# A seven-product cross-attention kernel: other signs in the sums, the softmax sum folded from T3, product 6 of y in blocks, and an earlier place for GpSimd's sums

## The chip, the cores and the metric

The kernel runs on one core of a Trainium2 chip. The metric is the device time of one execution in microseconds (us). The core's engines work side by side, each through its own list of instructions: TensorE (PE in the profile, with its weight loads as PEld) does matrix products into PSUM, VectorE (DVE) works on pairs of tensors, ScalarE (ACT) copies, scales and takes exponentials, GpSimd (POOL) reduces over partitions and issues DMAs that can add to their target, and SyncE (SP) issues plain DMAs. GpSimd's DMAs are the queue q0 of the profile and SyncE's are q1.

## The reference

There are eight batches. For each of them, in fp32:

```python
q = einsum('bcn,dc->bnd', x1, Wq) + bq                 # x1: 512 x 1024, q: 1024 x 64
k = einsum('bcn,dc->bdn', x2, Wk) + bk[:, None]        # x2 = ctx: 512 x 1024, k: 64 x 1024
v = einsum('bcn,dc->bdn', x2, Wv) + bv[:, None]        # v: 512 x 1024
attn = softmax(einsum('bnd,bdm->bnm', q, k), axis=2)   # 1024 x 1024
out = einsum('bcm,bnm->bcn', v, attn) + x1
```

## The kernel before

**What is computed.** The value projection comes after the attention: with e the exponentials of the scores less their maximum, laid out as m x n, the kernel computes y = x2 · e (512 x 1024 x 1024), divides y by the sums of e over m, and then forms out = Wv · y + bv + x1 (512 x 512 x 1024). In these words "context" is x2, its transposed blocks are the tiles `a`, and the weights are `w`.

**The seven-product form.** Both large products, "y" (context times e) and "o" (Wv times y), are cut into 2 x 2 blocks and done with seven block products in place of eight, in Winograd's form. The left factors are 11, 12, 22 and the sums S1 to S4, the right ones 11, 21, 22 and the sums T1 to T4. A table gives for each product its factors, its PSUM banks and whether it opens them; products that do not open a bank add to what stands there:

```python
MULT = {1: ("11", "11", "a", True), 2: ("12", "21", "c", True), 6: ("S2", "T2", "a", False),
        7: ("S3", "T3", "c", True), 5: ("S1", "T1", "a", False), 3: ("S4", "22", "a", False),
        4: ("22", "T4", "c", False)}
```

Blocks of e carry half 0 or 1 of the n columns as their second index, and half 0 or 1 of the m rows as their first: 11 and 21 belong to half 0, 12 and 22 to half 1. Before the change S1 = 21 + 22, S2 = 11 - S1, S3 = 11 - 21, S4 = 12 + S2 on the left (`left_sums`, lines 101 to 111), and T1 = 12 - 11, T2 = T1 - 22, T3 = 22 - 12, T4 = 21 + T2 on the right (`right_sums`, line 317). For y the left sums are those of the context, new in every batch: S1 is loaded (line 155) and added to by a DMA (159), S3 and S2 are negated on ACT (167) and added to by a DMA (171), and S4 is a DVE sum (108). T3 is made in place, on ACT and by a DMA (341, 342), T4 by copies on ACT and a DMA (330, 336).

**Two ways of doing one product.** `multiply` (line 420, matmuls at 437) is the plain one: per 128 rows of the result, four matmuls of 512 columns. `multiply_seeded` (lines 595 to 628) cuts the block product once more into seven, over 256 columns each, in the order 1, 7, 6, 2, 5, 4, 3 (its "steps"): steps 1, 6 and 5 chain in one PSUM tile (`ps_i...chain`), step 7 has its own (`ps_i...third`), ACT copies the chain's states into the banks (line 611) and step 7 into an SBUF tile `v`, and `complete` on DVE adds `v` to the second bank (626). Such a product needs sums of its own: four of the left factor, `left_stream` (line 485, tiles `aI`), and three passes for the right one, `right_stream` (500 over 1024 elements, 505 and 507 over 512 each; tiles `eI`). The digit in `ps_i5chain` or `eI7yT` is that of the product. Before the change all products of y are done in this way in batches 2 to 8, except product 6; batch 1 does 1, 2 and 6 plain. In the o stage product 7 is in blocks, woven with the plain 5 and 3 (`multiply_57`, lines 545 to 593); 1, 6, 2 and 4 are plain.

**One period.** `period` (line 868 on) writes the work for batch s from product 1 of its y to the last eviction of its output, with the scores and the softmax of the next batch n between, and loads for the ones after that (nn, nnn). A manual schedule holds: each engine executes its instructions strictly in the order in which they are written. The code numbers batches 0 to 7, the text 1 to 8. `five` stands for the batches in the middle: neither the first nor the last two. The order of PE in a middle period is product 1, 2, 6 of y, the scores of half 0 of batch n, products 5, 7, 3, the scores of half 1 and the keys of later batches, product 4, and then the o stage: 1, 6, 2, the woven 5, 7, 3, and 4. The periods meet at product 1.

**Softmax.** For each half h, DVE folds the maximum over four score tiles (`fold`, line 248), POOL takes it over the partitions (`highest`, 264), DVE subtracts it (`lower`, 299; tiles `e<-e,top`), ACT takes the exponential (308), and the sum of e over m comes from three fold passes on DVE or, for half 0, from DMAs that add (`add_tile`, 724), from a last fold of the two halves of the tile, and from POOL's all-reduce (`total`, 266 to 273). `invert` and `spread` (275 to 284) bring the reciprocal to all partitions, `scale_y` (648) multiplies y by it.

**Evictions.** `evict_y` (652) and `evict_t3` (638) form y's blocks from banks and the copies `u1`, `u6`, `u7`; `evict_o` (670 to 721) adds bias, copies and banks to the output tile, POOL then adds x1 by DMA (720), and SP stores it (721). Both DMAs are written right behind the eviction. `uo5` (tag `u5`) is the copy of product 5 of the o stage, into which block 22 of the output is built.

Of the kernel before, what the change touches and what calls it, by code (L numbers as in the profile page):

```python
# [15 lines left out]
def kernel(  # L16
# [84 lines left out]
    def left_sums(a, *ks):  # L101

        for k in ks:
            if k == "S3":
                nc.vector.tensor_tensor(a["21"], a["11"], a["21"], ALU.subtract)
                a["S3"] = a["21"]
            elif k == "S4":
                nc.vector.tensor_tensor(a[k], a["12"], a["S2"], ALU.add)
            else:
                x, y, op = {"S1": ("21", "22", ALU.add), "S2": ("11", "S1", ALU.subtract)}[k]  # L110
                nc.vector.tensor_tensor(a[k], a[x], a[y], op)
# [154 lines left out]
    def total(s, h):  # L266
        fold_halves(s, h, ALU.add)
        s.den[h] = sb.tile([P, H], F32, tag="den", name=f"den_{s.b}_{h}", bufs=2)
# [45 lines left out]
    def right_sums(t, k):  # L314

        x, y = {"T1": ("12", "11"), "T2": ("T1", "22"), "T3": ("22", "12"), "T4": ("21", "T2")}[k]
        nc.vector.tensor_tensor(t[k], t[x], t[y], ALU.add if k == "T4" else ALU.subtract)
# [8 lines left out]
    def copy_t4(s):  # L326

        s.t["T4"] = t4 = sb.tile([P, MH, H], F32, tag="eT4", name=f"eT4_{s.b}")
        for i in (0, 2):
            nc.scalar.copy(t4[:, i : i + 2, :], s.t["21"][:, i : i + 2, :])  # L330
# [7 lines left out]
    def sum_t3(s, i):  # L338

        t3 = s.t["T3"][:, i : i + 2, :]  # L340
        nc.scalar.mul(t3, t3, -1.0)
        nc.gpsimd.dma_start(t3, s.t["22"][:, i : i + 2, :], accum_op=ALU.add)

    def copy_u1(s, j):
        if j == 0:
            s.tmp[1] = sb.tile([P, 2, H], F32, tag="yT1", name=f"uy1_{s.b}")
        nc.scalar.copy(s.tmp[1][:, j, :], s.bank["a", j])
# [51 lines left out]

    def iter_t4(s):  # L400
        sum_y(s, "T4")
        yield
# [126 lines left out]
    def inner_parts(s, i):  # L529

        ks = ("third", "chain") if i in (2, 7) else ("chain", "third")
        of = {k: ps_s.tile([P, 2, H], F32, tag="sc", name=f"ps_i{i}{k}_{s.b}")[:, 0, left] for k in ks}
        return of["chain"], of["third"]
# [61 lines left out]
    def multiply_seeded(s, i, v_tag, hooks={}, bank=None):  # L595
# [11 lines left out]
        v = sb.tile([P, 2, H], F32, tag=v_tag, name=f"v{i}_{s.b}")[:, 0, left]  # L607
# [16 lines left out]
        def complete():  # L624
            b = b1.rearrange("p (a n) -> p a n", a=2)
            nc.vector.tensor_tensor(b, b, v.unsqueeze(1).to_broadcast([P, 2, H // 2]), ALU.add)
# [6 lines left out]
    def copy_7(s, j):  # L633
        if j == 0:
            s.tmp[7] = sb.tile([P, 2, H], F32, tag="u1", name=f"uy7_{s.b}")
        nc.scalar.copy(s.tmp[7][:, j, :], s.bank["c", j])
# [15 lines left out]
    def evict_y(s, k):  # L652

        bank, add = RESULT[k]
        if k == "22" or s.b == B - 1 and k == "21":
            bank, add = "a", 6
        s.y[k] = y = sb.tile([P, 2, H], F32, tag=f"y{k}", name=f"y{k}_{s.b}")
        for j in range(2):
            nc.vector.tensor_tensor(y[:, j, :], s.bank[bank, j], s.tmp[add][:, j, :], ALU.add)
# [10 lines left out]
    def evict_o(s, k):  # L670
# [37 lines left out]
        if add is None:  # L708
            o = sb.tile([P, 2, H], F32, tag="u1" if k == "11" else "r", name=f"r{k}_{s.b}")
            for j in range(2):  # L710
                nc.scalar.activation(o[:, j, :], s.bank[bank, j], AF.Identity, bias=bias(j))  # L711
        else:
# [6 lines left out]
        if k != "21":  # L719
            nc.gpsimd.dma_start(o, block(s, k, x1), accum_op=ALU.add)  # L720
        nc.sync.dma_start(block(s, k, out), o)
# [146 lines left out]
    def period(s, n, nn, nnn):  # L868
# [25 lines left out]
        def scores_0():  # L894
            then = scores_and(n, 0, 1 if nn else 2, "c", next_queries if nn else nothing)
            if nn is None:
                first(6, (1,))
            if s.b:
                for i in range(1, MH):
                    fold(n, 0, i, "max", ALU.max)  # L900
                highest(n, 0)
            return then
# [4 lines left out]

        def first_sum():
# [3 lines left out]
        open_t(s)  # L912
        if s.b == 0:
# [6 lines left out]
            s.a["S4"] = sb.tile([P, MH, C // 2], F32, tag="aS4", name=f"aS4_{s.b}")  # L920
            nc.scalar.copy(s.a["S4"], s.a["S2"])
            nc.gpsimd.dma_start(s.a["S4"], x2T[s.b, 0, 1], accum_op=ALU.add)
# [12 lines left out]
            for i in range(1, MH):  # L935
                fold(s, 1, i, "sum", ALU.add)
            total(s, 1)
            sum_e(s, "T3")
            weave(right_stream(s, 5, s.t["T1"], "y21", "u5"))
# [25 lines left out]
        else:  # L965
            complete_1 = multiply_seeded(s, 1, "y11")
            sum_e(s, "T1", "T2")
            complete_1()
            sums_5 = left_stream(s, 5, s.a["S1"], "i2"), right_stream(s, 5, s.t["T1"], "y21", "u1")
            if n:  # L970
                weave(folds(s, 1, "sum", ALU.add), left_stream(s, 7, s.a["S3"], "yT4"))
                total(s, 1)
                invert(s, 0)
            else:
                weave(folds(s, 1, "sum", ALU.add), left_stream(s, 7, s.a["S3"], "yT4"))
                weave(*sums_5)
            complete_2 = multiply_seeded(
                s, 2, "y22", {5: lambda: copy_u1(s, 0), 4: lambda: copy_u1(s, 1)}
            )
            sum_t3(s, 0)  # L980
            sum_t3(s, 2)
            if n is None:
                total(s, 1)
            complete_2()
            evict_y(s, "11")
            copy_t4(s)
            add_t4(s)
            first(6, (0,) if n and nn is None else range(2))
            if n:
                weave(*sums_5)  # L990
            if n:
                sum_a(s, "S4")
                evict_q = scores_0()
                spread(s, 0)
                shares(s, 1)
            if n:
                weave(right_stream(s, 7, s.t["T3"], "yT1", "yT2"), left_stream(s, 3, s.a["S4"], "aI3"))
            else:
                sum_a(s, "S4")
                weave(right_stream(s, 7, s.t["T3"], "yT1", "yT2"), left_stream(s, 3, s.a["S4"], "aI3"))  # L1000
                invert(s, 0)
                spread(s, 0)
# [4 lines left out]
            if n is None:  # L1007
                shares(s, 1)
            if n:
                weave(right_stream(s, 3, s.t["22"], "eT1"), lowers(n, 0, 0, 1))  # L1010
# [8 lines left out]
            if n:  # L1019
                lower(n, 0, 1)  # L1020
            complete_3 = multiply_seeded(s, 3, "r", hooks, "c")
# [6 lines left out]
            if n:  # L1028
                for i in range(2, MH):
                    lower(n, 0, i)  # L1030
            complete_3()
            evict_t3(s)
        if n:
            if s.b:
                load_a(n, "11")
            begin_s1(n)
# [15 lines left out]
            end_s1(n)  # L1052
            if nn:
                next_keys()
        if late and n:
            weave(left_stream(s, 4, s.a["22"], "a12"), right_stream(s, 4, s.t["T4"], "eT2"))
        if late:
            scale_y(s, "11", "T3", "22")
# [3 lines left out]
        if five:  # L1062
            weave(folds(n, 1, "max", ALU.max))
# [8 lines left out]
        if five:  # L1072
            highest(n, 1)
        complete_4()
        if late and n:
            negate(n, "S3")
# [10 lines left out]
        scale_y(s, "21")  # L1087
        if s.b == 0:
# [4 lines left out]
        if five:  # L1093
            weave(iter_t4(s), right_stream(s, "o7", s.y["T3"], "eT1"))
# [4 lines left out]
        if late and n and not five:  # L1099
            weave(folds(n, 1, "max", ALU.max), right_stream(s, "o7", s.y["T3"], "eT1"))  # L1100
# [11 lines left out]
        second(6)  # L1112
        if n:
# [8 lines left out]
        evict_o(s, "11")  # L1122
        if n:
            if not five:
                add_tile(n, 0, 3)
            if late:
                inner_left(n, 1, n.a["11"], "i2")
        if late:
            complete_7, rest = multiply_57(s)
        else:  # L1130
# [4 lines left out]
        if n:  # L1135
            for i in range(MH) if s.b else (2,):
# [5 lines left out]
        if n:  # L1142
            negate(n, "S2")
            add_11(n, "S2")
        evict_o(s, "22")
# [3 lines left out]
        if n:  # L1149
            weave(  # L1150
                right_stream(n, 1, n.e[0][:, 0], "yT1", "yT2"), left_stream(n, 2, n.a["12"], "aS4")
# [4 lines left out]
            evict_o(s, "12")  # L1156
# [46 lines left out]
```

## Time and profile before

| what | value |
|---|---|
| median of 3 runs | 677.41 us (676.89 to 677.58) |
| the profiled execution's own time | 677.15 us |
| its span in the profile | 675.4 us |
| largest groups of DVE: lowering the scores (299) | 60 instructions, 70.6 us |
| folding (248), maximum alone | 30 instructions, 36.7 us |
| exponentials on ACT (308) | 60 instructions, 61.5 us |
| POOL's all-reduces: sums (269), maxima (264) | 52.5 us and 31.0 us |
| plain y products and product 6 (437, `ps_ya<-eT,aS`) | 112 matmuls, 49.5 us |

The span goes from the first to the last instruction; the execution's own time is 1.75 us longer. An engine's "busy" time says nothing of who sets the time, since engines run side by side; that is read from what each waits for, stage by stage. In what follows, a line of a "windows" view gives for a stretch of the span its length, then each engine's busy time with the number of instructions, the clock that was granted to TensorE (1.00 is full), the mean busy share of the 16 DMA engines, and GB/s. A line of a "groups" view gives the source line, engine, operation and tile, the count, the busy time, the mean duration in ns, and the idle time ahead with what ended it. A line of a "timeline" view gives start and busy time in us, engine, line, operation, tiles, the count, and in square brackets the wait ahead of it and what ended that.

### The profile page before, as it was taken

How to read it: one execution, taken by the hardware profiler on the slowest of the kernel's cores; microseconds unless marked ns; L12 is line 12 of the kernel's file. 1: busy time of each engine (PE TensorE's matmuls, PEld its weight loads, DVE VectorE, ACT ScalarE, POOL GpSimd, SP SyncE). 2: the span in 40 equal slices, each digit the busy share in tenths (PEclk: the TensorE clock that was granted, in tenths of full speed). 3: DMA queues.
4: the chain of work that ended last, by engine and by line, in shares of the span. 5: the costliest groups of instructions: out<-in, count | busy, mean ns of one | idle time of the engine just before them, and what ended most of it. 6: DMA issues, size and time to landing. Idle time of an engine off the chain costs nothing.

```text
span 675.4 us, 7565 instructions
## 1 busy us (share of the span) xinstructions
PE 666.4 (99%) x2510; PEld 413.1 (61%) x2510; DVE 612.5 (91%) x811; ACT 358.5 (53%) x619; POOL 218.2 (32%) x188
## 2 busy tenths in 40 slices
PE   8999999999999999999999999999999999999996
PEld 5334754766556665657656486574855757566853
DVE  1999999999999889998999979999899989999984
ACT  3755456366465464654745647445565456565321
POOL 0126206260344411642134411445122460153400
PEclk9999999999999999999999999999999999999999
DMA  9678798958997959969599695996969968489412
GB/s 304 272 207 278 190 264 152 247 116 245 249 212 192 196 172 301 173 184 249 152 276 190 179 267 151 240 214 175 270 108 222 218 136 231 94 154 251 80 42 98
DMA packets 51638, 134.26 MB, mean 199 GB/s; under 512 B 5648, under 2 KB 7952, under 8 KB 51600
## 3 DMA queue, kind: packets, MB, share of 16 engines
q0 software_dynamic: 23328, 57.75, 47.9%
q1 hardware_dynamic: 27984, 75.64, 31.0%
q10 hardware_dynamic: 288, 0.39, 0.2%
q8 instruction: 20, 0.33, 0.2%
q14 instruction: 18, 0.15, 0.1%
HBM read 88.35 MB, written 16.81 MB: 156 GB/s over the span
## 4 chain that ended last, share of the span: by engine, by line
PE 87%; DVE 7%; DMA 3%; POOL 1%; issue 1%; SPq 1%; ACT 0%; DVEq 0%; POOLq 0%
PE ps_yc L518 10%; PE ps_ya L437 7%; PE ps_oa L559 6%; PE ps_ya L518 5%; PE ps_oa L437 5%; PE ps_s L228 5%; PE ps_o L437 4%; PE ps_oc L437 4%; PE ps_o L457 4%; PE ps_q L181 4%; PE ps_k L181 3%; PE ps_i4chain L518 3%; PE ps_i5chain L518 3%; PE ps_i7chain L518 3%; PE ps_i3chain L518 3%; PE ps_i1chain L518 2%
## 5 line engine op out<-in xcount | busy, mean ns | idle before, releaser
L269 POOL PARTITION_ALL_REDUCE den<-sum x16 | 52.5, 3283 | 72.7 <-DVE few L277 52.6
L724 POOL DMA_DIRECT2D sum<-e x21 | 27.9, 1328 | 145.7 <-ACT sum L729 71.6
L299 DVE TENSOR_TENSOR e<-e,top 128x1024 f32<-128x1024 f32 x60 | 70.6, 1218 | 0.4 <-POOL top L264 0.4
L308 ACT ACTIVATE e<-e 128x1024 f32<-128x1024 f32 x60 | 61.5, 1055 | 8.4 <-DVE e L299 7.8
L237 ACT COPY e<-ps_s 128x1024 f32<-128x1024 f32 x46 | 45.7, 1031 | 8.3 <-PE ps_s L228 8.3
L437 PE MATMUL ps_ya<-eT,aS 128*128 128x512 f32 x112 | 49.5, 593 | 0.0
L228 PE MATMUL ps_s<-q,k 64*128 64x512 f32 x188 | 47.5, 609 | 0.8 <-ACT q L751 0.8
L264 POOL PARTITION_ALL_REDUCE top<-max x16 | 31.0, 1940 | 52.1 <-DVE few L277 20.4
L248 DVE TENSOR_TENSOR max<-max,e 128x1024 f32<-128x1024 f32 x30 | 36.7, 1225 | 2.5
L437 PEld LDWEIGHTS ps_ya<-eT,aS 128*128 128x128 f32 x112 | 21.2, 190 | 24.1 <-issue 23.5
L284 POOL DMA_DIRECT2D den<-row x16 | 9.0, 561 | 78.0 <-DMA row<-few 75.0
L228 PEld LDWEIGHTS ps_s<-q,k 64*128 64x128 f32 x188 | 16.8, 186 | 24.8 <-issue 16.3
L720 POOL DMA_DIRECT2D r<-in_x_dram x14 | 29.3, 2090 | 2.9 <-ACT r L711 2.9
L648 DVE TENSOR_TENSOR y<-y,den 128x1024 f32<-128x1024 f32 x24 | 29.3, 1220 | 0.2
L437 PE MATMUL ps_o<-y,w 128*128 128x512 f32 x64 | 28.8, 592 | 0.0
L457 PE MATMUL ps_o<-y,w 128*128 128x512 f32 x64 | 28.8, 592 | 0.0
L437 PE MATMUL ps_oa<-yT,w_S 128*128 128x512 f32 x64 | 28.8, 592 | 0.0
L437 PE MATMUL ps_oc<-yT,w 128*128 128x512 f32 x64 | 28.8, 592 | 0.0
L611 ACT COPY ps_yc<-ps_i7chain 128x256 f32<-128x256 f32 x32 | 11.4, 357 | 30.3 <-PE ps_i7chain L518 22.3
L611 ACT COPY ps_ya<-ps_i5chain 128x256 f32<-128x256 f32 x32 | 11.4, 358 | 29.9 <-PE ps_i5chain L518 25.7
L485 DVE TENSOR_TENSOR aI<-a,aI 128x256 f32<-128x256 f32 x60 | 26.0, 433 | 1.0
L611 ACT COPY ps_ya<-ps_i1chain 128x256 f32<-128x256 f32 x28 | 10.0, 357 | 30.6 <-PE ps_i1chain L518 27.0
(257 smaller groups left out, 1734.8 us busy)
## 6 DMA issues: line engine op xcount, KB each, us to landing
x_in_x_dram<-in_x_dram SPq DMA_DIRECT2D x60, 512.0 KB, 9.3
a<-in_x2T_dram SPq DMA_DIRECT2D x32, 512.0 KB, 9.5
sum<-e POOLq DMA_DIRECT2D x21, 512.0 KB, 7.5
eT<-eT POOLq DMA_DIRECT2D x16, 512.0 KB, 10.9
aS<-in_x2T_dram POOLq DMA_DIRECT2D x15, 512.0 KB, 7.4
uo<-in_x_dram POOLq DMA_DIRECT2D x14, 512.0 KB, 9.6
r<-in_x_dram POOLq DMA_DIRECT2D x14, 512.0 KB, 11.5
out_dram<-r SPq DMA_DIRECT2D x14, 512.0 KB, 3.4
```

The source lines that it names most:

```text
L181: nc.tensor.matmul(ps[r, :], w_sb[:, c, :], s.x[:, c, ts(h, H)], start=(c == 0), stop=(c == CT - 1),)
L228: nc.tensor.matmul(ps[g], s.k[r, ts(i, P)], s.q[r, ts(h, H)], start=True, stop=True)
L237: nc.scalar.copy(e[:, :, i, :], whole)
L248: nc.vector.tensor_tensor(f, e[:, :, 0, :] if i == 1 else f, e[:, :, i, :], op)
L269: nc.gpsimd.partition_all_reduce(s.den[h], s.mx[h][:, 0, :], P, ReduceOp.add)
L299: nc.vector.tensor_tensor(e, e, top, ALU.subtract)
L308: nc.scalar.activation(e, e, AF.Exp)
L437: nc.tensor.matmul(ps[:, n], left[ka][:, k, ts(j, P)], right[kb][:, k, n], start=opens and k == 0, stop=i in (2, 3, 4) and k == n_k - 1, s ...
L457: nc.tensor.matmul(ps, w["11"][:, k, ts(j, P)], s.y["11"][:, k, :], start=k == 0, stop=False, skip_group_check=True)
L518: nc.tensor.matmul(ps, s.inner[i][ka][:, k, :], s.inner[i, "t"][kb][:, k, :], start=opens and k == 0, stop=z in (2, 3, 4) and k == n_k - 1 ...
L559: nc.tensor.matmul(ps[:, n], w[ka][:, k, ts(j, P)], s.y[kb][:, k, n], start=False, stop=i == 3 and k == 1, skip_group_check=True,)
L611: nc.scalar.copy(out, of)
```

## The change

It has four parts.

1. *Signs.* The second block column of the context and the second block row of e carry the opposite sign inside the form: S1 = 21 - 22, S2 = 11 - S1, S4 = 12 - S2; T1 = 12 - 11, T2 = T1 + 22, T3 = 22 + 12, T4 = T2 - 21. S1 is now begun by ACT's negation of 22 and not by a load. T3 needs no negation. The copies of T4 and of product 7 are negated, and the eviction of 21 subtracts.
2. *The sum of half 1.* T3 = 22 + 12 is already the sum of both row blocks of half 1; `sum_1` folds it in one DVE pass and the last fold of halves, in place of three passes over four tiles.
3. *Product 6 in blocks.* In batches 3 to 6 (`s.six`) product 6 of y goes through `multiply_seeded`. It has its own `left_stream` and `right_stream`; S4 is made by ACT's negation of S2 and a DMA that adds, ACT copies `uy6` behind the scores (`copy_u6`), a DMA adds `uy1` to it, and the closing addition works on `uy6`. `uy1` and some sums move to other tiles.
4. *Order.* In the middle batches the next batch's T1 and the DMAs for T3 are written in the output stage, ahead of the eI1 sums and of the x1 additions of blocks 22 and 12. These two additions and their stores leave `evict_o` as functions (`leave`); that of 22 is called behind T3's DMAs, that of 12 in the next period behind T2. The exponentials of half 1 are taken earlier: two during the eviction of block 11, two behind `multiply_57`. The lowering of the scores, the scaling of y and the folds change places; so do the sums for product 4 in batch 7 and the reciprocal of half 0 in batch 8.

```diff
-            nc.vector.tensor_tensor(a[k], a["12"], a["S2"], ALU.add)
+            nc.vector.tensor_tensor(a[k], a["12"], a["S2"], ALU.subtract)
...
+            self.six = 2 <= b < B - 2
...
+    def copied_s4(s):
+        s.a["S4"] = sb.tile([P, MH, C // 2], F32, tag="aS4", name=f"aS4_{s.b}")
+        nc.scalar.mul(s.a["S4"], s.a["S2"], -1.0)
+    def add_s4(s):
+        nc.gpsimd.dma_start(s.a["S4"], x2T[s.b, 0, 1], accum_op=ALU.add)
     def begin_s1(s):
-        nc.sync.dma_start(s.a["S1"], x2T[s.b, 1, 0])
+        nc.scalar.mul(s.a["S1"], s.a["22"], -1.0)
     def end_s1(s):
-        nc.gpsimd.dma_start(s.a["S1"], x2T[s.b, 1, 1], accum_op=ALU.add)
+        nc.gpsimd.dma_start(s.a["S1"], x2T[s.b, 1, 0], accum_op=ALU.add)
...
+    def sum_1(s):
+        t = s.t["T3"]
+        s.mx[1] = sb.tile([P, 2, H], F32, tag="fold", name=f"sum_{s.b}_1", bufs=2)
+        nc.vector.tensor_tensor(s.mx[1], t[:, 0:2, :], t[:, 2:4, :], ALU.add)
+        fold_halves(s, 1, ALU.add)
+    def total_1(s):
+        sum_1(s)
+        reduce_total(s, 1)
...
     def sum_t3(s, i):
         t3 = s.t["T3"][:, i : i + 2, :]
-        nc.scalar.mul(t3, t3, -1.0)
         nc.gpsimd.dma_start(t3, s.t["22"][:, i : i + 2, :], accum_op=ALU.add)
+    def copy_u6(s, j):
+        if j == 0:
+            s.tmp[6] = sb.tile([P, 2, H], F32, tag="u6", name=f"uy6_{s.b}")
+        nc.scalar.copy(s.tmp[6][:, j, :], s.bank["a", j])
...
-        if k != "21":
-            nc.gpsimd.dma_start(o, block(s, k, x1), accum_op=ALU.add)
-        nc.sync.dma_start(block(s, k, out), o)
+        def leave():
+            if k != "21":
+                nc.gpsimd.dma_start(o, block(s, k, x1), accum_op=ALU.add)
+            nc.sync.dma_start(block(s, k, out), o)
+        if hook is None and k in ("12", "22"):
+            return leave
+        leave()
...
+            if s.six:
+                copy_u6(s, 0)
+                copy_u6(s, 1)
+                nc.gpsimd.dma_start(s.tmp[6], s.tmp[1], accum_op=ALU.add)
+                add_t4(s)
+                weave(folds(n, 0, "max", ALU.max), right_stream(s, 7, s.t["T3"], "yT1", "yT2"))
...
+        def while_11(j):
+            if five:
+                exponential(n, 1, j)
+            elif j:
+                early_s2()
...
-            complete_1 = multiply_seeded(s, 1, "y11")
-            sum_e(s, "T1", "T2")
-            complete_1()
+            complete_1 = multiply_seeded(s, 1, "y11", {4: lambda: copied_s4(s)} if s.six else {})
+            if s.b == 1:
+                complete_1()
+            early = s.b > 1 and n is not None
+            sum_e(s, *(("T2",) if early else ("T1", "T2")))
+            if s.b > 1:
+                complete_1()
...
+            for leave in s.leave:
+                leave()
...
+            if s.six:
+                add_s4(s)
+                weave(left_stream(s, 6, s.a["S2"], "i2"), right_stream(s, 6, s.t["T2"], "yT2", "y21"))
...
+            if s.six:
+                complete_6 = multiply_seeded(
+                    s, 6, "top", {6: lambda: copy_t4(s, (0,)), 4: lambda: copy_t4(s, (2,))}
+                )
+            else:
+                copy_t4(s)
+                add_t4(s)
+                first(6, (0,) if n and nn is None else range(2))
...
+            if s.six:
+                complete_6(s.tmp[6][:, 1, :])
             complete_3 = multiply_seeded(s, 3, "r", hooks, "c")
...
+        leave = evict_o(s, "22")
+        if n and nn is None:
+            exponentials(n, 1, 2)
+            exponentials(n, 1, 3)
+            early_s2()
+        if five:
+            open_t(n)
+            sum_e(n, "T1")
+            sum_t3(n, 0)
+            sum_t3(n, 2)
+        if five:
+            leave()
...
-            evict_o(s, "12")
+            last = evict_o(s, "12")
+            n.leave = [last] if five else [leave, last]
```

More of the change, by code (lines that the diff above doesn't have):

```diff
@@ L919, in period @@
             fold(s, 0, 3, "sum", ALU.add)
[L920 to L922 removed]
+            copied_s4(s)
+            add_s4(s)
             copy_t4(s)
@@ L934, in period @@
             parts_6(s, 2)
-            for i in range(1, MH):
-                fold(s, 1, i, "sum", ALU.add)
-            total(s, 1)
             sum_e(s, "T3")
+            total_1(s)
             weave(right_stream(s, 5, s.t["T1"], "y21", "u5"))
@@ L1087, in period @@
         scale_y(s, "21")
+        if five:
+            scale_y(s, "22")
         if s.b == 0:
@@ L1135, in period @@
         if n:
-            for i in range(MH) if s.b else (2,):
+            for i in () if five else (0, 1) if s.b else (2,):
                 exponentials(n, 1, i)
```

169 lines of the change are left out of this document (105 added, 64 removed).

## The prediction

> **What bounds the kernel now.** I read the page's busy times first, then busy time per batch, then what TensorE waited for, then the order of time inside one batch.
>
> ```profile
> span 675.4 us, 7565 instructions
> PE 666.4 (99%) x2510; PEld 413.1 (61%) x2510; DVE 612.5 (91%) x811; ACT 358.5 (53%) x619; POOL 218.2 (32%) x188
> ```
>
> Busy time by batch (first batch, then batches 3, 4, 7 and 8; the cuts lie at the start of product 6):
>
> ```profile
> core 0: us, PE busy (x) PEld busy (x) DVE busy (x) ACT busy (x) POOL busy (x), PEclk, DMA share, GB/s
> 24.88:130.28 105.40, 105.40 (x373) 58.64 (x374) 103.18 (x126) 59.10 (x94) 34.94 (x27) 1.00 0.82 213
> ...
> 211.97:293.55 81.58, 81.58 (x312) 51.51 (x311) 75.05 (x101) 45.67 (x81) 28.27 (x24) 1.00 0.85 208
> 293.55:375.13 81.58, 81.58 (x312) 51.51 (x311) 75.50 (x101) 45.67 (x81) 28.23 (x24) 1.00 0.85 211
> ...
> 538.29:614.48 76.19, 75.53 (x280) 49.15 (x279) 72.78 (x98) 43.07 (x76) 28.49 (x24) 1.00 0.75 166
> 614.48:675.40 60.92, 55.37 (x195) 36.13 (x193) 48.77 (x74) 18.78 (x40) 9.52 (x10) 0.98 0.39 104
> ```
>
> In the middle batches PE is busy for the whole 81.58 us at full clock, and two periods agree to 0.01 us: PE work taken out there comes off the time, as long as DVE (75.5 of 81.58 us) still delivers. Batch 7 has 0.66 us of PE idle, and PE's waits name its cause:
>
> ```profile
> PE ps_i4third L518 <- DVE eI4eT L500: 0.4, 1, 0.4
> PE ps_i4chain L518 <- DVE aI L485: 0.2, 1, 0.2
> ```
>
> **The change, part by part.** *Product 6 in blocks* (batches 3 to 6). Windows over the plain product 6, and over products 2 and 5, which have the seven-block form already:
>
> ```profile
> 374.97:381.93 6.96, 6.96 (x18) 2.85 (x16) 6.92 (x12) 4.57 (x6) 3.22 (x1) 1.00 0.45 172
> 368.93:374.97 6.04, 6.04 (x30) 5.32 (x28) 6.04 (x7) 2.61 (x7) 0.60 (x1) 1.00 1.08 270
> 389.15:395.30 6.15, 6.15 (x31) 5.42 (x30) 4.31 (x9) 3.08 (x7) 2.80 (x3) 1.00 1.05 202
> ```
>
> 6.04 us is the product alone, 6.15 us with the change between 64-row and 128-row matmuls, which stays at the scores behind product 6. So 6.96 - 6.15 = 0.81 us per batch, four batches: **-3.24 us**. Ends: 0.92 x 4 = 3.68 if the change of form costs nothing there; below, zero, if the other engines stall PE for as much.
>
> *Does DVE still deliver?* Rows of the fourth batch's groups, the block sums from the whole run:
>
> ```profile
> L248 DVE TENSOR_TENSOR sum<-sum,e 128x1024 f32<-128x1024 f32 x3 | 3.6, 1212 | 0.0
> L317 DVE TENSOR_TENSOR eT<-e,e 128x1024 f32<-128x1024 f32 x2 | 3.3, 1696 | 0.0
> L341 ACT ACTIVATE e<-e 128x1024 f32<-128x1024 f32 x3 | 3.2, 1066 | 0.9 <-DVE sum L248 0.9
> L317 DVE TENSOR_TENSOR eT<-eT,e 128x1024 f32<-128x1024 f32 x2 | 2.3, 1212 | 0.0
> L485 DVE TENSOR_TENSOR aI<-aS 128x256 f32<-128x256 f32 x4 | 2.1, 520 | 0.0
> L485 DVE TENSOR_TENSOR aI<-aS,aI 128x256 f32<-128x256 f32 x4 | 1.7, 415 | 0.0
> L626 DVE TENSOR_TENSOR ps_ya<-ps_ya,v 128x512 f32<-128x512 f32 x2 | 1.4, 693 | 0.1
> L500 DVE TENSOR_TENSOR eI5y<-eT 128x1024 f32<-128x1024 f32 x1 | 1.2, 1214 | 0.0
> L108 DVE TENSOR_TENSOR aS<-a,aS 128x1024 f32<-128x1024 f32 x1 | 1.2, 1212 | 0.0
> ...
> L505 DVE TENSOR_TENSOR eI5u<-eI5y,eT 128x512 f32<-128x512 f32 x8 | 5.4, 680 | 0.0
> ```
>
> Out per batch: two of three sum passes (T3 is folded once instead of four tiles), 2 x 1.212, and S4's sum, 1.212: -3.64. In: four left sums (2 x 0.520 + 2 x 0.415), three right sums (1.214 + 2 x 0.680), the closing addition of product 6 (0.693): +5.14. DVE gets +1.5, 77.0 of 80.77 us, 95%: it fits, with 3.8 us to spare instead of 6.1. ACT loses two negations (2 x 1.066), gains five block copies (about 0.36 each) and S4's and S1's negations (1.07 each, as the row of negations): +1.8 on 45.7, no bound. Signs alone (subtract for add) I cost at nothing: same row, same shape.
>
> *Who is late next?* The orders on DVE, ACT and PE, batch 5's start, as they are now:
>
> ```profile
> 357.08 1.41 DVE L716 SCALAR_TENSOR_TENSOR uo<-ps_oc,bv_sb,uo 128x512 f32<-128x512 f32 x2 [0.20 <-PE ps_oc L518]
> 358.40 1.22 DVE L500 TENSOR_TENSOR eI1yT<-e 128x1024 f32<-128x1024 f32 x1
> ...
> 391.88 1.23 DVE L500 TENSOR_TENSOR eI7yT<-e 128x1024 f32<-128x1024 f32 x1 [1.80 <-DMA e<-e]
> ```
>
> ```profile
> 356.05 3.90 ACT L308 ACTIVATE e<-e 128x1024 f32<-128x1024 f32 x4
> ...
> 368.26 0.36 ACT L611 COPY ps_ya<-ps_i1chain 128x256 f32<-128x256 f32 x1 [0.51 <-PE ps_ya L518]
> 369.99 0.36 ACT L611 COPY ps_yc<-ps_i2chain 128x256 f32<-128x256 f32 x1 [1.37 <-PE ps_i2chain L518]
> ```
>
> ```profile
> 364.61 1.03 PE L518 MATMUL ps_i1chain<-eI1yT,aI 128*128 128x256 f32 x4
> ...
> 396.16 1.03 PE L518 MATMUL ps_i7third<-eI7yT,aI 128*128 128x256 f32 x4
> ```
>
> T1 (two `eT<-e,e`) now stands ahead of eI1yT at 358.40, and waits for the last exponential. Two of the four exponentials move ahead into the output stage, so ACT ends them at about 356.05 + 2 = 358.1. T1 then takes 2.4 us at the 1212 ns of its sister row, 3.4 at 1696. The sums eI1yT, one aI and half of the next (1.2 + 0.4 + 0.7) end at 363.1 or 364.1; PE asks at 364.61: 0.5 to 1.5 us left, no stall. T1's 1696 against 1212 ns is the overlap with the all-reduce of the sums, which stood beside it and comes later now; I take 1212. [...]
>
> Behind it T2 and product 6's sums run gap-free and end before PE's steps by about 1 us. Product 7's sums gain: eI7yT waited 1.80 us for the sum of T3 by DMA, 4 us ahead of PE's step. That DMA now starts some 20 us earlier.
>
> *ACT and the queues.* S4's negation (1.07) goes between the copies at 368.26 and 369.99, a gap of 1.37 us, and reads S2, which an added DMA completes:
>
> ```profile
> 361.19 0.90 POOL L171 DMA_DIRECT2D aS<-in_x2T_dram x1 [5.39 <-ACT aS L167]
> ...
> 364.79 0.39 SPq L721 DMA_DIRECT2D out_dram<-r  x1
> ...
> q0 software_dynamic: 23328, 57.75, 47.9%
> q1 hardware_dynamic: 27984, 75.64, 31.0%
> ```
>
> Q0 takes 0.479 x 675.4 us for 57.75 MB, 2.9 us per 512 KB sum; q1 1.45 us per 512 KB. SP's output at 364.79 waited for the sum queued ahead of S2's, so S2 lands at about 367.7, 0.9 us before ACT wants it. Per batch two POOL sums come in (S4, and uy6 += uy1) and one SP load goes (S1): +4.4 us of DMA on 0.85 x 81.58, a share of 0.91. The new sums are wanted 9 us or more after their issue. GpSimd's moved DMAs (T3's ahead of `uo5`'s, x1's late) release output tiles by 3 to 4 us later; SP waits for these, and DVE meets `u5` again some 20 us on.
>
> *The batches without product 6.* Batch 7 loses two sum passes and has T1 done early: most of its 0.66 us of idle goes, but the lowering of the last scores now waits for the maximum's all-reduce before product 7 of the output is closed: take **-0.5** (0 to -0.7). Batch 1 loses 2.4 us of sums ahead of product 5, whose steps run late, and batch 8 ahead of product 7:
>
> ```profile
> 62.84 1.03 PE L518 MATMUL ps_i5third<-eI5y,aI 128*128 128x256 f32 x4
> 63.81 1.13 PE L518 MATMUL ps_i5chain<-eI5u,aI 128*128 128x256 f32 x4
> ...
> 627.37 1.03 PE L518 MATMUL ps_i7chain<-e,a 128*128 128x256 f32 x4
> 628.46 1.10 PE L518 MATMUL ps_i7third<-eI7yT,aI 128*128 128x256 f32 x4
> 629.39 1.10 PE L518 MATMUL ps_i7chain<-eI7yT,aI 128*128 128x256 f32 x4
> ```
>
> A step is 6.04/7 = 0.86 us; four of 0.97 in batch 1 are 0.4 us, 1.09 and 0.93 in batch 8 are 0.3 us: **-0.6** together (0 to -0.7).
>
> Sum: the profiled execution took 677.15 us, 0.26 below the runs' median. 677.15 - 3.24 - 0.5 - 0.6 = 672.8; with 0.26, 673.1. I say **673.0 us**.
>
> **Rivals.** *Part of it is given back.* At 95% DVE has little to catch up with: 0.3 us of PE wait per batch in batches 2 to 6 and nothing won in 1, 7, 8 give 677.4 - 3.2 + 1.5 = 675.7. For: slacks of about 1 us. Against: no wait of PE in four batches at 92%.
>
> *Slower: ACT held by S2's sum.* S4's negation stands before product 2's copies in ACT's order. If S2 lands after 369.0, these copies slip, and past 0.3 us more PE's third step does. The gain per batch is gone when it lands 1.1 us after that, at 370.1. One 512 KB sum served ahead of it (2.9 us) makes 370.6, about even at 678; two make 373.5, 4.2 us x 4 = 17 us: 690 us. For: the DMA share at 0.91. Against: S2 is issued ahead of T3's sums in the same queue.
>
> *Slower: T1 late.* Each us past its slack costs five starts; from 1.1 us past it the whole is 0.2% slower, 679.
>
> *Weight loads come into the open.* Product 6 goes from 16 loads (2.85 us) to 28 (5.32). Unhidden, that is 2.47 x 4 = 9.9 us, 684 us. Against it speak the windows: 5.32 us of loads inside a product of 6.04 us without a gap. [...] Hence 0.01.
>
> **How the numbers follow.** Forecast 0.56 (its own range 672.3 to 674.4), partly given back 0.24 (to 676.0), stalls that equal the gain 0.05, S2's sum 0.08, T1 0.05, weight loads 0.01, an unseen wait 0.01. 0.2%, 1.35 us, is about what a measurement tells from no change. Faster 0.80, same 0.05, slower 0.15. The range of 671.8 (every term at its far end, 677.4 - 3.68 - 0.7 - 0.7 = 672.3, and the medians' scatter) to 677.6 leaves out the slower cases.
>
> **What would show it.** Right: periods of 80.77 us in batches 3 to 6, PE busy all through, DVE 77 us, no PE wait in batch 7 at product 4. Wrong: PE waiting for an ACT copy of product 2 (S2's sum), for eI1yT (T1), or PE steps over 0.87 us in product 6.

## The result and the profile after

The changed kernel takes 683.97 us (683.17 to 684.77) where the kernel before takes 677.25 us in the same comparison: a ratio of 1.0099, with an interval of 1.0082 to 1.0117. It is 6.7 us slower; 673.0 us was forecast, with 677.6 us as the upper end.

First the head of the page after:

```profile
span 682.6 us, 7705 instructions
PE 668.1 (98%) x2558; PEld 425.3 (62%) x2558; DVE 607.1 (89%) x823; ACT 363.4 (53%) x636; POOL 226.8 (33%) x196
```

PE is busy for 1.7 us longer and idle for 5.5 us longer, although the blocks took work out of it. Where that lies is read from the periods. The windows are cut at product 1 of batches 2 to 8; first the kernel before (batch 2, one middle batch, 7 and 8), then the changed one (all seven):

```profile
118.03:199.72 81.69, 81.69 (x311) 51.88 (x310) 77.55 (x106) 45.65 (x79) 26.89 (x25) 1.00 0.87 214
199.72:281.30 81.58, 81.58 (x311) 51.51 (x310) 75.05 (x101) 45.67 (x79) 28.27 (x26) 1.00 0.84 207
...
526.04:602.24 76.20, 75.54 (x280) 49.15 (x279) 73.86 (x99) 43.53 (x76) 28.50 (x26) 1.00 0.73 164
602.24:675.40 73.16, 67.61 (x251) 46.91 (x249) 59.88 (x86) 22.89 (x51) 15.02 (x14) 0.98 0.51 124
```

```profile
119.32:209.75 90.43, 84.97 (x312) 54.17 (x311) 76.58 (x102) 44.85 (x78) 31.77 (x27) 0.96 0.82 196
209.75:290.50 80.75, 80.75 (x323) 53.78 (x322) 75.94 (x106) 47.50 (x84) 30.01 (x27) 1.00 0.90 218
290.50:371.89 81.39, 81.03 (x323) 53.70 (x322) 75.94 (x106) 47.59 (x84) 30.03 (x27) 1.00 0.90 216
371.89:452.65 80.76, 80.76 (x324) 53.78 (x322) 76.25 (x106) 47.49 (x84) 30.02 (x27) 1.00 0.91 218
452.65:533.40 80.75, 80.75 (x323) 53.78 (x322) 75.93 (x106) 47.50 (x84) 30.03 (x27) 1.00 0.89 200
533.40:608.60 75.20, 75.15 (x279) 49.39 (x278) 69.56 (x96) 41.55 (x74) 24.49 (x21) 1.00 0.69 159
608.60:682.60 74.00, 67.92 (x251) 46.83 (x249) 59.13 (x87) 22.24 (x52) 16.86 (x15) 1.00 0.53 127
```

Batches 3, 5 and 6 show what the forecast said: 80.75 instead of 81.58 us, PE busy throughout. Batch 7 is 1.00 us shorter. Against this stand batch 2 with +8.74 us, batch 4 with 0.64 us above its neighbours, batch 8 with +0.84 us and the part ahead of batch 2 with +1.29 us (119.32 against 118.03). Together 1.29 + 8.74 - 2.67 - 1.00 + 0.84 = 7.2 us, the difference of the spans. One batch, which has no product 6 in blocks at all, lost more than everything else won.

What PE waited for, in the changed kernel:

```profile
PE ps_i5chain L544 <- ACT ps_ya L640: 5.5, 1, 5.5
...
PE ps_i4third L544 <- DVE eI4eT L526: 1.0, 1, 1.0
...
PE ps_i3chain L544 <- ACT ps_yc L640: 0.4, 1, 0.4
```

The first of these is batch 2's. The timelines of PE, ACT, SP and POOL there tell the chain backwards; the second block has the same rows of POOL, SP and ACT in the kernel before:

```profile
155.08 2.08 PE L544 MATMUL ps_i5chain<-eI5y,aI 128*128 128x256 f32 x4 [5.46 <-ACT ps_ya L640]
156.94 1.91 PE L544 MATMUL ps_ya<-eI5u,aS 128*128 128x256 f32 x4
...
154.38 0.37 ACT L640 COPY v<-ps_i5third 128x256 f32<-128x256 f32 x1 [6.90 <-DMA out_dram<-r]
154.65 0.38 ACT L640 COPY ps_ya<-ps_i5chain 128x256 f32<-128x256 f32 x1
...
145.87 0.37 SPq L756 DMA_DIRECT2D out_dram<-r  x1
...
131.10 2.39 POOL L755 DMA_DIRECT2D r<-in_x_dram  x1
```

```profile
117.16 1.20 POOL L720 DMA_DIRECT2D r<-in_x_dram  x1 [0.52 <-ACT r L711]
...
131.62 0.37 SPq L721 DMA_DIRECT2D out_dram<-r  x1
...
146.44 0.37 ACT L611 COPY v<-ps_i5third 128x256 f32<-128x256 f32 x1 [0.45 <-PE ps_i5third L518]
```

Block 12's output tile and the tile `v` of product 5 share one buffer, tag `r`. ACT copies step 7 into `v` and has to wait until the old `r` is stored. Its x1 addition was issued at 117.16 us and is now issued at 131.10 us, in the next period behind T2 and the DMAs for T3. It takes about as long as before to land (14.8 us against 14.5 us until SP can store), so the store comes 14 us later. The store itself then takes 8.4 us from issue to landing, where it took 2.9 us; the mean busy share of the DMA engines is 1.05 in the 10 us from 145 us on. In the kernel before it had landed some 12 us ahead of ACT's copy. Behind the waiting ACT stands the copy that PE needs (154.65). PE's next steps then take 1.7 to 1.9 us and not 0.86; the granted clock is 0.50 in these 5.28 us (last column but two):

```profile
155.08:160.36 5.28, 5.28 (x13) 4.20 (x14) 0.78 (x2) 1.94 (x4) 0.00 (x1) 0.50 1.04 327
```

5.46 us of wait and half of 5.28 us are 8.1 of the 8.74 us. In batch 4 DVE met `u5` before its store had landed, in batch 8 product 4's sums waited for T4:

```profile
314.63 1.22 DVE L526 TENSOR_TENSOR eI5u<-eT 128x1024 f32<-128x1024 f32 x1 [4.38 <-DMA out_dram<-uo]
...
646.96 1.23 DVE L526 TENSOR_TENSOR eI4eT<-eT 128x1024 f32<-128x1024 f32 x1 [1.25 <-DMA eT<-eT]
```

```profile
634.47 0.58 POOL L303 DMA_DIRECT2D row<-few  x1
637.32 0.54 POOL L308 DMA_DIRECT2D den<-row  x1 [2.28 <-DMA row<-few]
637.85 1.85 POOL L362 DMA_DIRECT2D eT<-eT  x2
```

On POOL, T4's DMAs (637.85) stand behind the broadcast `den<-row`, which waited 2.28 us for the row to land. In the kernel before they stood ahead of both, at 627.97 us:

```profile
627.97 1.77 POOL L336 DMA_DIRECT2D eT<-eT  x2
```

### The profile page after: what moved, and what is told of

The parts are those of the page before. It is cut to its first block, busy times and chain, and to the rows that moved or that the text cites. A ratio compares the mean times of both kernels' runs of the same rounds, so it can differ in the third digit from the quotient of the medians.

```text
span 682.6 us, 7705 instructions
## 1 busy us (share of the span) xinstructions
PE 668.1 (98%) x2558; PEld 425.3 (62%) x2558; DVE 607.1 (89%) x823; ACT 363.4 (53%) x636; POOL 226.8 (33%) x196
## 4 chain that ended last, share of the span: by engine, by line
PE 78%; DMA 11%; DVE 4%; POOL 2%; issue 2%; ACT 2%; SPq 0%; DVEq 0%; POOLq 0%; ACTq 0%
PE ps_yc L544 9%; PE ps_ya L544 6%; PE ps_s L238 5%; PE ps_oa L463 5%; PE ps_oa L585 5%; PE ps_o L463 4%; PE ps_o L483 4%; PE ps_oc L463 4%; PE ps_k L191 3%; PE ps_i4chain L544 3%; PE ps_q L191 3%; PE ps_i3chain L544 2%; DMA uo<-in_x_dram 2%; PE ps_i5chain L544 2%; PE ps_i7chain L544 2%
## 5 line engine op out<-in xcount | busy, mean ns | idle before, releaser
L293 POOL PARTITION_ALL_REDUCE den<-sum x16 | 53.4, 3340 | 75.9 <-DVE sum L268 75.9
L511 DVE TENSOR_TENSOR aI<-a 128x256 f32<-128x256 f32 x60 | 25.7, 449 | 0.0
L191 PE MATMUL ps_q<-x_in_x_dram,wqk_sb 128*64 128x512 f32 x112 | 25.6, 598 | 0.0
```

What stands on the lines that cost most here:

```text
L191: nc.tensor.matmul(ps[r, :], w_sb[:, c, :], s.x[:, c, ts(h, H)], start=(c == 0), stop=(c == CT - 1),)
L511: nc.vector.tensor_tensor(v[k], v[x], v[y], op)
```

## Experiments

The theory, A: tiles and transfers that the new order releases later hold ACT or DVE, and these hold PE; nothing is wrong with the blocks. The rival, B: the DMAs that the blocks add (share 0.90 in place of 0.85) crowd the queues, and the stall of batch 2 is only where this shows.

**Batch 1's outputs leave at once.** The two deferred functions are called in batch 1.

```diff
-        if five:
+        if five or s.b == 0:
             leave()
...
-            n.leave = [last] if five else [leave, last]
+            n.leave = [last] if five else [] if s.b == 0 else [leave, last]
+            if s.b == 0:
+                last()
```

> Only the outputs 22 and 12 of batch 1 change: their x1 additions and stores are issued right behind their evictions, as in the kernel before, and not in batch 2 behind the DMAs for T3. Theory A, the late store of `r`: the 5.46 us wait of TensorE in batch 2 and the slow steps behind it go, 8.7 us in all, so 684.0 - 8.7 = 675.3 us, period 2 at 81.6 to 81.8 us, granted clock at full. Rival B, the DMAs that product 6's blocks and S4 add crowd the queues (share 0.90) and the stall is only where this shows: the wait moves to another place, and the time stays above 680 us.

Measured: 680.23 us (676.86 to 683.96), ratio 1.0044 (1.0022 to 1.0066). The wait for `r` is gone, but another took its place in batch 2, whose period in the profiled execution (676.86 us) is 85.35 us:

```profile
PE ps_sc L238 <- DVE y L691: 2.7, 1, 2.7
```

```profile
134.93 0.18 DVE L301 RECIPROCAL few<-few 128x4 f32<-128x4 f32 x1 [4.38 <-DMA few<-den]
...
138.21 0.69 DVE L531 TENSOR_TENSOR eI5u<-eI5y,eT 128x512 f32<-128x512 f32 x1 [1.30 <-DMA out_dram<-r]
```

PE waits for the eviction of y's block 11, which on DVE stands behind the reciprocal of half 0 and product 5's sums. The reciprocal waits for `few`, and a tile of the sums is block 11's old output (tag `u1`), whose store is late as well. Here `few` takes 7.6 us from issue to landing, in the changed kernel it took 1.9 us and DVE did not wait for it. In the kernel before DVE had three folding passes at this place and reached the reciprocal only at 136.06 us, later than `few` lands here. A alone said 675.3 us and was too simple; by this run alone B, which said above 680 us, is as good.

**Product 6 plain again**, all else as in the change (`self.six = False`).

> The changed kernel with product 6 of y plain in all batches; signs, folded sum and order stay. Theory A: the stall of batch 2 has nothing to do with product 6 and stays; four periods lose 0.83 us of gain and batch 4 its wait of 0.6: 684.0 + 3.3 - 0.6 = 686.7 us. Rival B: with product 6's sums and DMAs gone, the stall is gone or halved: 677 to 680 us.

Measured: 685.53 us (684.79 to 685.94), ratio 1.0117 (1.0097 to 1.0137). The stall of batch 2 is there with 5.4 us. The blocks don't cause it, and neither do their DMAs.

**Three places mended.** To batch 1's outputs come the order of `uo5` and that of T4:

```diff
         if five:
+            leave()
             open_t(n)
             sum_e(n, "T1")
...
-        if five:
+        if s.b == 0:
             leave()
...
-            if n is None:
-                spread(s, 0)
...
                 add_t4(s)
+                if n is None:
+                    spread(s, 0)
```

> The changed kernel with three places mended: batch 1's outputs leave at once; in batches 2 to 6 the x1 addition of `uo5` is issued ahead of T3's DMAs; in batch 8 T4's DMAs are issued ahead of the broadcast of half 0's reciprocal. Theory A: 675.3 less 0.64 (batch 4) less 1.0 to 1.3 (batch 8) = 673.0 to 673.7 us, no wait of DVE for the store of `uo`, none of TensorE for eI4eT. If the earlier addition of `uo5` makes T3 late instead, DVE waits at the folded sum and the time is 675 us or more. Rival B: 677 us or more.

Measured: 679.38 us (677.07 to 682.06), ratio 1.0027 (1.0007 to 1.0046). The periods of batches 2, 4 and 8 in the profiled execution:

```profile
118.46:205.11 86.65, 83.95 (x311) 52.47 (x310) 76.21 (x102) 45.16 (x78) 30.36 (x26) 0.98 0.86 204
285.87:366.62 80.75, 80.75 (x323) 53.78 (x322) 75.71 (x106) 47.50 (x84) 30.07 (x27) 1.00 0.90 218
603.34:676.10 72.76, 67.68 (x251) 46.89 (x249) 59.05 (x87) 22.24 (x52) 16.85 (x15) 0.99 0.54 129
```

Batch 4 is at 80.75 us, batch 8 gains 1.24 us and is now 0.40 us shorter than before the change. Both did what was expected. Batch 2 still has its second wait, and the total misses the 673 us that were expected; it lies where B put it, at 677 us or more.

**The same with product 6 plain.**

> The same three places mended, and product 6 of y plain in all batches. The difference to the mended kernel with blocks is what the blocks are worth. Theory A: 4 x 0.83 = 3.3 us more than that kernel, 676.3 to 677.0 us: the rest of the change together is worth a few tenths. Rival B: the same time as with blocks, or less.

Measured: 688.64 us (682.80 to 690.51), ratio 1.0151 (1.0103 to 1.0198). It did not measure what it was meant to. With product 6 plain, product 5's sums stand ahead of product 2's closing addition in every middle batch, and there DVE meets the unstored `u1` up to 4.6 us early. This version has a stall of its own.

**Batch 2's second wait.** In the version with three places mended, POOL's last addition for the sum of half 0 in batch 1 waits for an exponential, and block 11's x1 addition waits behind it. It goes back behind that, and the reciprocal behind the eviction of y's block 11:

```diff
-        if s.b == 0:
-            add_tile(n, 0, 3)
...
-            if not nn:
+            if not five:
                 add_tile(n, 0, 3)
...
-            if n and not early:
-                invert(s, 0)
...
-            if early or n is None:
-                invert(s, 0)
+            invert(s, 0)
```

> The kernel with three places mended, and two more for batch 2: the DMA that adds the last tile to the sum of half 0 is issued in batch 1 behind block 11's eviction, as in the kernel before (it waits for an exponential, and block 11's x1 addition waited behind it), and batch 2 takes the reciprocal of half 0 behind the eviction of y's block 11 and not ahead of product 5's sums. Theory A2, DVE is held in batch 2 by the landing of two transfers (the sum row `few`, the store of block 11 from tile u1) and passes this on to TensorE: both come sooner or are met later, TensorE's 2.7 us wait and the slow steps behind it go, period 2 falls from 86.65 to 81.6 us, 672.8 us in all. Rival B2, the queue is too full at that place whatever the order: another wait of 2 us or more stays in batch 2, 676 us or more.

Measured: 674.42 us (674.14 to 677.07), ratio 0.9969 (0.9951 to 0.9987): faster than both kernels, and between the two expectations. The 2.7 us wait is gone; one of 0.86 us in product 2 of batch 2 is left, where DVE waits 2.3 us for the last addition to the sum of half 0.

**Only the reciprocal moved**, the POOL order as in the change.

> The kernel with three places mended, and of the two others only the later reciprocal in batch 2. If the wait for `few` was the cause, period 2 falls to about 82 us and the time to 673 us. If the tile u1 is what counts, DVE comes to it earlier and waits there until the same moment: TensorE's wait stays at 2 to 2.7 us and the time at that of the kernel with three places mended, 677 to 681 us. A2 says the second.

Measured: 680.17 us (680.11 to 681.38), ratio 1.0051 (1.0036 to 1.0066). As A2 said, DVE now waits longer at the next obstacle, and PE's wait even grew, from 2.7 to 4.9 us:

```profile
140.49 0.69 DVE L531 TENSOR_TENSOR eI5u<-eI5y,eT 128x512 f32<-128x512 f32 x1 [8.03 <-DMA out_dram<-r]
```

So the store of `u1` has to come first; taking a wait out ahead of it brings nothing (680.17 against 679.38 us). Against this version, POOL's old order is worth 5.8 us (680.17 to 674.42). POOL's order without the later reciprocal was not tried.

**Product 5's sums in the old place in batch 2**, added to the version of 674.42 us (`weave(*sums_5)` behind product 6 in all middle batches, as batches 3 to 6 already have it).

> As the kernel with both batch 2 places mended, and product 5's sums of batch 2 stand behind product 6 again, as in the kernel before: u1 is met some 8 us later. A2: no wait of DVE for a store in batch 2, period 2 at 81.6 us, 672.5 to 673.0 us.

The same with product 6 plain in all batches:

> The same with product 6 of y plain in all batches and product 5's sums behind it, so that no tile is met earlier than in the kernel before. The difference to the one with blocks is their worth, free of the stalls: 4 x 0.83 = 3.3 us, 675.8 to 676.3 us, periods of 81.58 us in batches 3 to 6. If the blocks' gain is given back by crowded queues, the difference is under 1.5 us.

Measured: 674.46 us (674.24 to 675.57) with blocks, ratio 0.9960 (0.9946 to 0.9975), and 677.49 us (676.76 to 678.21) with product 6 plain, ratio 1.0004 (0.9995 to 1.0014). The blocks are worth 3.0 us, near the 3.3 us expected. Batch 3 with blocks and plain:

```profile
202.00:282.75 80.75, 80.75 (x323) 53.78 (x322) 75.72 (x106) 47.49 (x84) 30.08 (x27) 1.00 0.91 218
```

```profile
201.63:283.21 81.58, 81.58 (x312) 51.51 (x311) 73.43 (x99) 44.88 (x78) 28.31 (x25) 1.00 0.81 198
```

The old place alone did not bring the 672.5 us expected: the wait in product 2 of batch 2 stays, so it lies elsewhere.

**S2's DMA in the old place**, again from the version of 674.42 us, with product 5's sums where the change has them. In batch 1 the DMA that completes the next S2 stands there ahead of the last sum and of block 11's x1 addition; it goes back behind product 7 of the output.

```diff
             if five:
                 exponential(n, 1, j)
-            elif j:
-                early_s2()
...
             second(7)
+            early_s2()
```

> The kernel with five places mended, and the DMA that completes batch 2's S2 stands behind product 7 of batch 1's output again, as in the kernel before, so that the last sum of half 0 and block 11's x1 addition are not queued behind it. A2: DVE's 2.3 us wait for that sum falls to 1.0 us, TensorE's 0.86 us wait in product 2 of batch 2 goes, period 2 falls from 82.99 to 81.6 us, 672.7 to 673.0 us. If the queue is full there anyway, 674.4 us as without it.

Measured: 672.85 us (672.09 to 673.04), ratio 0.9932 (0.9917 to 0.9947). As expected. No wait above 0.2 us is left on PE behind batch 1, with as many DMAs as in the change (the share in the middle batches is still 0.90 to 0.91): rival B falls. What the queues carry in all was not the trouble, but in which order, and what was met before it had landed. The folding passes are still out of DVE here, and it waits neither for `few` nor for the store of `u1` in batch 2.

**The queries of batch 1 evicted later**, inside product 5.

```diff
-            if five:
+            if five or s.b == 0:
                 return evict
...
-            complete_5 = multiply_seeded(s, 5, "r")
+            complete_5 = multiply_seeded(s, 5, "r", {6: evict_q})
```

> The same, and in batch 1 ACT evicts the next queries inside product 5 (behind its step 6), as the later batches do, and not ahead of it. The prediction laid the steps of 0.97 us in batch 1's product 5 to late sums on DVE; the trace of the changed kernel shows the same steps with the sums early, and weight loads that wait for ACT's copy behind the queries' eviction. If ACT is the cause, the steps fall to 0.86 us and the time by 0.3 to 0.4 us, to 672.4 us; if not, nothing changes.

Measured: 672.37 us (672.06 to 672.61), ratio 0.9927 (0.9912 to 0.9942), the fastest version. In the changed kernel the weight loads of product 5 in batch 1 had waited for ACT:

```profile
65.11 0.73 PEld L544 LDWEIGHTS ps_i5chain<-eI5u,aI 128*128 128x128 f32 x4 [0.35 <-ACT ps_ya L640]
```

Now the steps of that product are 0.86 us apart:

```profile
63.33 1.03 PE L544 MATMUL ps_i5third<-eI5y,aI 128*128 128x256 f32 x4
64.19 1.03 PE L544 MATMUL ps_i5chain<-eI5u,aI 128*128 128x256 f32 x4
65.06 1.03 PE L544 MATMUL ps_ya<-eT,aS 128*128 128x256 f32 x4
```

**Only the deferral put back** into the kernel of 672.85 us.

> The kernel of the first of these three runs, and only batch 1's two outputs are deferred again into batch 2, as in the change. If the late store of `r` is by itself the cause of the loss, TensorE waits 5 us or more in product 5 of batch 2, steps behind it are slow, and the time is 8 to 9 us longer, 681 to 682 us. If the stall needs the crowding by the other moves as well, it is 3 us or less.

Measured: 677.23 us (675.47 to 679.39), ratio 1.0000 (0.9987 to 1.0012). The deferral alone costs 4.4 us, between the two expectations: PE's wait for `r` is back, with 2.6 us in the profiled execution (675.67 us):

```profile
150.29 0.37 ACT L640 COPY v<-ps_i5third 128x256 f32<-128x256 f32 x1 [4.05 <-DMA out_dram<-r]
...
130.16 2.35 POOL L755 DMA_DIRECT2D r<-in_x_dram  x1
...
141.96 0.37 SPq L756 DMA_DIRECT2D out_dram<-r  x1
```

Here the x1 addition leads to the store in 11.8 us; in the changed kernel it took 14.8 us. The store takes 8.2 us, about as in the changed kernel. So the rest of that loss goes with the other moves in batches 1 and 2, in which this transfer is longer; which of them lengthens it was not separated.

**Two more passes on DVE** in batches 3 to 6 of the fastest version; they read T3 and write a tile that nothing reads.

```diff
+        if s.six:
+            spare = sb.tile([P, 2, H], F32, tag="fold", name=f"spare_{s.b}_1", bufs=2)
+            for _ in range(2):
+                nc.vector.tensor_tensor(spare, t[:, 0:2, :], t[:, 2:4, :], ALU.add)
```

> The kernel with all places mended and the queries evicted later; in batches 3 to 6 two more passes of the folded sum's size run on DVE behind the folded sum, into a tile that nothing reads, so that DVE has as much to do as with the three passes of the kernel before. By the totals, DVE has the room: 75.9 us of 80.76 are busy, two passes add 2.3, and nothing changes, 672.4 us. By the place, it has not: y's block 11 is evicted behind the passes and leaves its bank 1.5 us before TensorE writes scores there; 2.3 us of passes make TensorE wait 0.8 us in each of four batches, 675.6 us, and product 6's blocks win nothing. The prediction weighed the totals and a slack of about 1 us; I expect the second.

Measured: 677.93 us (676.26 to 680.07), ratio 1.0005 (0.9994 to 1.0015): 5.6 us more than without the passes by the medians of two comparisons, 5.3 us by their ratios to the kernel before. The period of batch 4, and PE's waits:

```profile
280.66:363.43 82.77, 81.62 (x324) 54.47 (x323) 78.16 (x108) 47.76 (x84) 30.10 (x27) 1.00 0.88 213
```

```profile
PE ps_sc L238 <- DVE y L695: 2.5, 3, 1.1
```

Without the passes DVE was busy for 75.7 to 76.3 of 80.75 us, with some 5 us of room, and PE still waits, at the place that was named; the loss is larger than the 3.2 us expected. The periods of batches 3 to 6 are together 5.7 us longer than without the passes, and the named waits are 2.5 us of that; where the rest arises was not followed. With the sum of half 1 as long as before, at this place, product 6's blocks win nothing.

## Why the prediction was wrong

- *The blocks, -3.24 us.* Right: 0.82 to 0.83 us in each of batches 3, 5 and 6, and 3.0 us between the two otherwise equal versions. Weight loads stayed hidden: 53.78 us of them in a period in which PE is busy throughout.
- *DVE still delivers, 77.0 us.* Right for the total (75.9 to 76.3 us), and the slack of about 1 us ahead of T1, T2 and product 6's sums held: no wait of PE there. But the rival "part is given back" was weighed by DVE's total share, and the last experiment shows that the place counts: 2.3 us of passes in a period with 5 us of room cost more than the blocks win.
- *S2's sum, the rival at 0.08, and T1, the rival at 0.05.* Neither came: ACT and PE wait for neither in batches 3 to 6. T1 ran at the shorter of the two durations, as taken (1213 ns each in batch 4), and T2 now shares its time with the all-reduce of the sums and takes 1696 ns each (DVE's and POOL's timelines of the changed kernel):

```profile
286.02 2.35 DVE L341 TENSOR_TENSOR eT<-e,e 128x1024 f32<-128x1024 f32 x2
...
296.60 3.31 DVE L341 TENSOR_TENSOR eT<-eT,e 128x1024 f32<-128x1024 f32 x2
...
295.46 3.23 POOL L293 PARTITION_ALL_REDUCE den<-sum  x1 [4.63 <-DVE sum L268]
```

In the kernel before it was T1 that stood beside the all-reduce and had the 1696 ns, while T2 behind it had 1212:

```profile
366.71 3.31 DVE L317 TENSOR_TENSOR eT<-e,e 128x1024 f32<-128x1024 f32 x2
...
369.95 2.35 DVE L317 TENSOR_TENSOR eT<-eT,e 128x1024 f32<-128x1024 f32 x2
...
365.58 3.23 POOL L269 PARTITION_ALL_REDUCE den<-sum  x1 [1.02 <-DVE sum L258]
```

- *"GpSimd's moved DMAs (...) release output tiles by 3 to 4 us later."* This step failed. It was worked out from the middle batches, where only block 12 goes into the next period, and used for all. In the middle batches too it was short: measured from product 1, the store of `u5` is issued some 7 us later than before in batch 4 (15.0 against 8.2 us) and some 6 us later in batch 6 (14.3 against 8.5 us). In batch 1 both outputs go, behind a T1 that is not early there, and the x1 addition of `r` is issued 13.9 us later. The text followed the tile `u5` to its next user, DVE, and did not ask who meets `r` next: ACT, with PE's copies queued behind it. At this wait 8.1 us are lost. The deferral by itself costs 4.4 us in the mended kernel, and taking it out of the changed one brings 3.7 us, for the next stall then shows. In batch 8, where both outputs of batch 7 come late in the same way, the changed kernel puts `v` of product 5 into a tile of another tag (`top`), and ACT waits for no store; that this would do for batch 2 was not tried. DVE waited for the store of `u5` in batches 4, 5 and 6, for 4.38, 2.81 and 2.85 us; in batch 4 this cost 0.64 us, where the step had costed it at nothing.
- *The same kind of miss in batches 2 and 8.* The moves on POOL in batch 1, the last sum of half 0 and S2's DMA ahead of block 11's x1 addition, stand in no term of the prediction. In the changed kernel DVE waits 2.29 us for the store of `u1`, without a wait of PE; once the outputs leave at once, this order costs more: putting it back brought 5.8 and 1.6 us. The fold passes taken out of DVE would have covered the late landing of `few` in the first experiment; the saving was booked and the cover was not. That the cover is needed is not shown, since without the passes no wait of PE above 0.2 us is left once POOL's order is back. In batch 8 POOL's broadcast went ahead of T4's DMAs, and of a step moved past a queue's other entries only DVE's side was costed: +0.84 us where -0.3 was put down. With T4's DMAs ahead again, batch 8 is 0.40 us shorter, near the estimate.
- *Batch 1, -0.4 us, by late sums.* The size was right (the last edit in batch 1 brought 0.48 us), but the cause was another, so this was luck. The steps of 0.97 us stayed with the sums early; they fell to 0.86 us when ACT's eviction of the queries moved. The row quoted for it was PE's; the weight loads' row would have named ACT. The +1.29 us ahead of batch 2 has two other parts. The first y product starts at 25.64 us instead of 24.88; in the other versions of the changed kernel it starts at 24.99 to 25.57 us, with no edit in that part, so much of this is scatter between executions, though all start later than the one of before. And PE loses 0.54 us at batch 1's keys, where it waits 0.32 us for the load of their input; no other version shows this wait.
- *Batch 7, -0.5 us.* Right in kind and too small; it measured -1.00 us, outside the 0 to -0.7 given: PE is idle for 0.61 us less and busy for 0.39 us less.

The sum of 673.0 us was that of a kernel without these stalls: with the orders put back, 672.85 us was measured, and 672.37 us with the queries moved as well. That 672.85 us comes so near is in part luck, since batch 1's gain is not in it and batch 7's is larger than was said.

## What to carry to other kernels

When a store or an addition is deferred, list for every tile it releases who writes that buffer next, on which engine, and what is queued behind that writer; do it for the first and last rounds of the loop separately, where other branches hold. Where a queue is worked in order, as POOL's was here (T4's DMAs stood behind a broadcast that waited 2.28 us), ask what stands behind a DMA that has to wait. When work is taken off an engine, ask which landing it covered: the engine may come to the same transfer sooner and wait, as DVE did for `few` in the first experiment (4.38 us). DVE's free time per period said little here (some 5 us of room, and 2.3 us of passes cost 5.3 to 5.6 us); look at the margin at the one place where another engine needs the result.

## What was not expected of the hardware

A wait of PE cost more than its length here. Behind the 5.46 us wait the granted clock was 0.50 for the next 5.28 us. Waits of 2.7 us came out in two ways: in the version with three places mended the clock fell to 0.75 over the 3.42 us around the wait's end, and the period grew to 86.65 us,

```profile
139.91:143.33 3.42, 1.99 (x5) 1.20 (x7) 3.35 (x8) 0.10 (x1) 0.00 (x0) 0.75 1.10 245
143.33:146.80 3.47, 3.47 (x13) 1.23 (x11) 3.44 (x5) 2.41 (x4) 0.24 (x1) 0.76 1.07 248
```

while with batch 1's outputs alone at once the same wait left the clock at full, with 85.35 us, as did one of 2.61 us in the version with only the deferral put back. The row is of the first of these two:

```profile
136.00:150.00 14.00, 11.33 (x44) 5.04 (x43) 12.59 (x18) 5.05 (x7) 5.10 (x3) 1.00 1.03 238
```

The versions with a wait of about 2.7 us in batch 2 scatter by 3.9 to 7.1 us over ten executions each, the two without a wait there (672.85 and 672.37 us) by under 1 us over four. The clock goes with it: with three places mended, the five longest executions (680.47 to 682.06 us) had a mean granted clock of 0.994, the other five (677.07 to 678.28 us) 0.996 or 0.997. What decides whether the clock falls is not shown: waits of 2.61 to 2.70 us went both ways.
